# Moving the ranking, the gathered queries and the attention's pace in a two-layer graph transformer

## The chip, the cores and the metric

The kernel runs on one core of a Trainium2 chip. The core has a matmul engine (PE), a vector engine (DVE), a scalar engine (ACT), a general engine (POOL), which here mostly issues gathers and scatters by row number, and SP, which issues plain transfers. Each engine works off its own instructions in order and waits on semaphores for the others. The metric is the device time of one execution, in microseconds (us): the median of several runs.

## The reference

Two layers of a graph transformer work on 2708 nodes with 512 features. Each layer computes, with eight heads of 64:

```python
q, k, v = h @ Wq.T + bq, h @ Wk.T + bk, h @ Wv.T + bv     # (n, 8, 64) each
scores = einsum('nhd,mhd->hnm', q, k) / sqrt(64)
scores = where(mask == 0, -1e9, scores)                    # mask: adjacency plus identity
ctx = einsum('hnm,mhd->nhd', softmax(scores), v)
h1 = layer_norm(h + ctx @ Wo.T + bo)
h2 = layer_norm(h1 + relu(h1 @ W1.T + b1) @ W2.T + b2)     # 2048 hidden features
```

The adjacency matrix is sparse: a node has only a handful of neighbours, so only those scores matter.

## The kernel before, in words

The nodes lie in 22 tiles of 128 rows, the last with 20. The kernel works by edges (`by_edges`): for each node it makes a list of its neighbours, sorts the nodes by the length of their lists ("rank"), and lets attention fetch, for a tile of 128 nodes of like rank, the key and value rows of one neighbour of each by a gather. `CAPS` gives how many neighbours a tile of ranks needs, from 22 for tile 0 down to 7, 6, 5 and 3 for tiles 18 to 21. Attention goes through the tiles in `order`: 21, 20, 19, 18, 8, 9 and so on, short lists first.

**Keys, values and lists (`first`).** For each of the 22 tiles of nodes in their natural order, PE multiplies by Wk and Wv, DVE adds the bias to k (L861), ACT copies v, and ACT's queue writes both to `kv_d` in memory. Beside it, DVE makes the lists from the rows of the adjacency matrix. `counted` then counts, and `ranked` (L738 on) makes each node's rank: four matmuls with a triangle and with ones, two products and sums on DVE, 22 scatters of list records on POOL into `rec_d`, loads of them back in order of rank, and `ident_i`, the node of each rank, for the four last tiles. `ranked` is called behind k of the last tile and ahead of its v (L863).

**Queries (`first_queries`).** For each tile of nodes PE multiplies by Wq; DVE scales and adds the bias into `qs` (L909), and SP writes pairs of tiles to `q_d`. Attention wants queries by rank. For tiles 21, 20 and 19 the kernel doesn't wait for `q_d`: `own_rows` gathers their rows of x by rank (POOL), `turned_own` transposes them (PE, then an ACT copy), and `own_query` multiplies by Wq again (PE, then DVE at L949). Tile 18 and all behind it are gathered out of `q_d` by `asked`, once all of `q_d` is written (`all_made`); until then attention stands still in front of tile 18. `OWN` = 10 says where this happens: after q of tile 9 `listed(True)` makes the gather numbers and the attention's first gathers start, after q of tile 10 come the transposes and the own queries of 21 and 20, after that of tile 12 the own query of 19.

**Attention (`attend`).** A step takes one chunk of two neighbours of a tile: DVE multiplies by q and sums (L1013, L1019), one step later ACT takes the exponential (L1032) and scales one neighbour's values (L1039) while DVE scales the other's and adds (L1045, L1052), and at the tile's end DVE sums and ACT divides into `cx` (L1083). A ring of five buffers (`KVB`) holds gathered chunks. Nothing runs attention by itself: `advance(x)` lets it go on by x chunks, at places in the emitted order; `through(k)` runs it until block k's `cx` is there. `beside_queries` does both during the queries: `advance` of 1.0 or 0.6 for each q behind `OWN`, `through(0)` at the 17th q (NT − 6), and the output projection of block 0 at the 18th.

**Feed-forward.** Blocks of two tiles: transposes of `cx`, the product with Wo (`o`), a norm, transposes of h, and then 16 times a product with W1 (`pf`, L1290), relu on ACT (`ft`, L1298) and, three steps behind, the product with W2 (`a`, L1278). Between these, attention for the next block advances; at step 11 of the first block of layer 0 `through(1)` demands block 1's `cx`. In layer 0 each finished block gets its keys and values for layer 1.

**The border.** Layer 1 starts with 16 queries. Eight have their transposed inputs preloaded (`pool`), the others load `zT` through SP, three at a time. DVE puts each into one of three `qs` buffers and SP writes them to `q_d`. Attention of layer 1 advances by 0.65 of a chunk for each of ten of them (the fifth to the fourteenth); then `through(0)` demands block 0 of layer 1, and the last two queries follow its projection.

**Order.** PE, ACT and SP keep the order in which the code emits their instructions, everywhere. POOL and DVE keep it only within the stretches put by hand (POOL: keys, queries and the first block of layer 0; DVE: queries of layer 0 and the border); elsewhere a planner orders DVE and POOL. `project` puts its result into one of three PSUM buffers named g, or, for `other=True`, into one of three named f.

Of the kernel before, what the change touches and what calls it, by code (L numbers as in the profile page):

```python
# [8 lines left out]
F32 = mybir.dt.float32  # L9
# [9 lines left out]
P = 128  # L19
DM = 512  # L20
# [17 lines left out]
QB = 3  # L38
# [4 lines left out]
XB, XBS = 256, 11  # L43
LEAD = 1.3
QT = 6
OWN = 10
EARLY = 3
FIRST = 4
PACE = (0.62, 0.72)
# [422 lines left out]
def by_edges(ctx: ExitStack, tc: tile.TileContext, x, xT, adj, layers, out, good):  # L472
# [11 lines left out]
    NT = (N + P - 1) // P  # L484
# [20 lines left out]
    own = {}  # L505
    all_made = []
    at = None
# [57 lines left out]
    def project(xs, r, wm, name, other=False):  # L565

        o = (ps_f if other else ps).tile([P, DM], F32, tag="f" if other else "g", name=name)
        for c in range(NC):
            nc.tensor.matmul(o[:r], xs(c), wm[:, c, :], start=(c == 0), stop=(c == NC - 1))  # L569
        return o  # L570
# [243 lines left out]
    def first(w, meanwhile):  # L814

        xg = []

        def load():
            i = len(xg)
            b = i % XBS * XB  # L820
            bw = min(XB, N - b)
            t = wts.tile([P, NC, XB], F32, tag=f"w1_{5 + i % 3}", name="xg")
            xg.append(t)
            step = bw if i else P
            for a in range(0, bw, step):
                nc.sync.dma_start(
                    out=t[:, :, a : a + step], in_=chunked(xT)[:, :, b + a : b + a + step]
                )
                yield

        def tokens(t, again):

            i, c0 = t * P // XB, t * P % XB
            if c0 == 0 and len(xg) < 2 * XBS:
                finish(load())
            xs = xg[i + again * XBS]
            return lambda c: xs[:, c, c0 : c0 + size(t)]

        wk = wts.tile([P, NC, DM], F32, tag="wk", name="wk")
        halves = load()  # L840
        next(halves)
        for c in range(NC):
            nc.sync.dma_start(out=wk[:, c, :], in_=chunked(w["Wk"])[:, c, :])
            if c == 0:
                cols = [given_column(w, "bk")]
        cols.append(given_column(w, "bq"))
        finish(halves)
        turning = turned_row(cols[0], "bk", 1.0)
        bk = next(turning)
        wv = matrix(w, "Wv", "wv")  # L850
        pa = tc.tile_pool(name="pa", bufs=2)
        lists, counted, ranked, listed = lists_of(pa.__enter__())
        done, before = 0, None
        for t in range(NT):
            r = size(t)
            xs = tokens(t, 0)
            kv = wts.tile([P, 2 * DM], F32, tag=f"w2_{5 + t % 3}", name="kvs")
            k = project(xs, r, wk, "k")
            if t == 0:
                finish(turning)  # L860
            nc.vector.tensor_tensor(kv[:r, :DM], k[:r], bk[:r], ALU.add)  # L861
            if t == NT - 1:
                ranked(*counts)  # L863
            v = project(xs, r, wv, "v", other=True)
            nc.scalar.copy(kv[:r, DM:], v[:r])
            if before:
                nc.scalar.dma_start(**before)
            before = dict(out=kv_d[0][t * P : t * P + r, :], in_=kv[:r])
            if t == 0:
                finish(load())  # L870
            while done < min(NT, 1 + LEAD * t):
                lists(done)
                done += 1
                if done == NT:
                    counts = counted()
            meanwhile(t)
            if t == QT:
                wq = matrix(w, "Wq", "wq")
                turning = turned_row(cols[1], "bq", DK**-0.5)
                bq = next(turning)  # L880
                finish(turning)
        nc.scalar.dma_start(**before)
        return bq, wq, listed, pa, tokens

    def first_queries(bq, wq, listed, pa, tokens, meanwhile):

        nonlocal at
        xrs = [own_rows(g) for g in order[:3]]
        made = []

        def written():
            t, qs = made.pop(0)
            if t + 2 < NT:
                out = q_d[0][t * P : (t + 2) * P, :].rearrange("(two p) c -> p two c", p=P)
                nc.sync.dma_start(out=out, in_=qs)
                return
            for i in range(2):
                r = size(t + i)
                nc.sync.dma_start(out=q_d[0][(t + i) * P : (t + i) * P + r, :], in_=qs[:r, i])

        for t in range(NT):
            r = size(t)
            if t % 2 == 0 and made:
                written()
            q = project(tokens(t, 1), r, wq, "q", other=t % 2 > 0)
            if t % 2 == 0:
                qs = wts.tile([P, 2, DM], F32, tag=f"w2_{5 + t // 2 % 3}", name="qs")
                made.append((t, qs))
            nc.vector.scalar_tensor_tensor(  # L909
                qs[:r, t % 2], q[:r], DK**-0.5, bq[:r], ALU.mult, ALU.add  # L910
            )
            if t == OWN - 1:
                listed(True)
                pa.__exit__(None, None, None)
                at = ctx.enter_context(tc.tile_pool(name="at", bufs=2))
                for g in order[:3]:
                    own[g] = at.tile([P, DM], F32, tag="q", name="q", bufs=QB)
                to = dict(own)
                next(ahead)
            if t == OWN:  # L920
                zTs = [turned_own(g, xr) for g, xr in zip(order, xrs)]
                for g, zT in zip(blocks[0], zTs):
                    own_query(g, zT, to[g], bq, wq)
                    advance(0.5)
            if t == OWN + 1:
                listed(False)
            if t == OWN + 2:
                own_query(order[2], zTs[2], to[order[2]], bq, wq)
            meanwhile(t)
        while made:  # L930
            written()
        all_made.append(True)

    def own_rows(g):
        r = size(g)
        xr = dn.tile([P, DM], F32, tag="row", name="xr", bufs=3)
        gather(xr[:r], x, ident_i[:r, g : g + 1])
        return xr

    def turned_own(g, xr):  # L940
        zT = dn.tile([P, NC, P], F32, tag="cT", name="zT", bufs=3)
        flip(xr, size(g), zT[:, :, : size(g)])
        return zT

    def own_query(g, zT, to, bq, wq):

        r = size(g)
        q = project(lambda c: zT[:, c, :r], r, wq, "q")
        nc.vector.scalar_tensor_tensor(to[:r], q[:r], DK**-0.5, bq[:r], ALU.mult, ALU.add)  # L949
# [418 lines left out]
    order = [g for block in blocks for g in block]  # L1368
# [49 lines left out]
    def advance(more):  # L1418

        nonlocal credit  # L1420
        credit = min(credit + more, 1.5)
        while credit > 0 and len(got) < CXB - 1:
            cost = next(ahead, None)
            if cost is None:
                break
            credit -= cost
# [19 lines left out]
    def beside_queries(t):  # L1446

        if t == 3:
            for total, other in sums:
                nc.vector.tensor_tensor(total, total, other, ALU.add)  # L1450
        if len(now.w2) < 5:
            now.load_w1(len(now.w1), nc.scalar)
            now.load_w2(len(now.w2), nc.scalar)
        if t > OWN:
            advance(1.0 if t < NT - 6 else 0.6)
        if t == NT - 6:
            through(0)
            early[0] = now.attended(blocks[0], got)
            next(early[0])
        if t == NT - 5:  # L1460
            for _ in blocks[0]:
                next(early[0])

# [8 lines left out]
    for n in range(NL):  # L1472
        last = n == NL - 1
        nxt = None if last else Layer(n + 1, layers[n + 1])
        if n > 0:
            streamed = now.queries(order[8 : 2 * AHEAD])
            got = {}
            ahead = attend(n, got)
            with tc.manual_schedule(engines={mybir.EngineType.DVE}):
                for _ in range(2):  # L1480
                    now.query(*pool.pop(0))
                next(ahead)
                next(streamed)
                while pool:
                    advance(0.65)
                    now.query(*pool.pop(0))
                for i in range(2 * AHEAD - 10):
                    advance(0.65)
                    next(streamed)
                through(0)  # L1490
                early[n] = now.attended(blocks[0], got)
                next(early[n])
                for _ in blocks[0]:
                    next(early[n])
                finish(streamed)
            now.load_w2(NFC // 2 - 1)
# [141 lines left out]
```

## Time and profile before

| what | value |
|---|---|
| median of three runs | 1971.49 us (1968.82 to 1974.34) |
| the profiled execution, and its span | 1975.51 us, 1973.8 us |
| mean granted clock of PE | 0.985 |
| PE busy | 1902.7 us, 96% |
| DVE busy | 1300.5 us, 66% |
| ACT busy | 933.5 us, 47% |
| POOL busy | 794.1 us, 40% |
| PE's waits for ACT's ft at pf, 3 of them | 9.9 us in all, 6.0 the longest |
| POOL's gathers waiting for DVE's acc | 313.5 us in all |

The profile is of one execution. "Busy" is the time in which an engine has an instruction; the span runs from the first instruction to the last, the execution has 1.7 us around it. Idle time of an engine that is not the bound costs nothing: POOL waits 313.5 us for buffers to come free and nobody need notice. An instruction's line names where it was made; helpers such as `project` (L569) and `gather` (L976) serve many callers, so one goes by the names of the tiles: `kv<-kv_d,idx` is a gathered chunk of attention, `q<-wq,xg` a query, `q<-wq,zT` an own query (layer 0) or a query of the border (layer 1), `tp<-ident,xr` the transposes of gathered rows.

### The profile page before, as it was taken

The numbers are of one execution on the slowest core, as the hardware profiler recorded it, in microseconds if no ns is written. First come the engines' busy times: TensorE is split into PE (matmuls) and PEld (weight loads), VectorE is DVE, ScalarE is ACT, GpSimd is POOL, SyncE is SP. The second block draws the span as 40 slices with busy tenths as digits, with TensorE's granted clock in tenths as the row PEclk, the third lists the DMA queues.
The fourth block names the chain that finished last, engine by engine and source line by source line (L and its number), as shares of the span: only waits on it lengthen the run. The fifth ranks groups of instructions, "written<-read, shape, count | busy, mean of one in ns | idle before, by whom it ended". The sixth has DMA issues, their size and how long they took to land. (4 is left out here: it accounts for less than half of the span.)

```text
span 1973.8 us, 20851 instructions
## 1 busy us (share of the span) xinstructions
PE 1902.7 (96%) x6150; PEld 1102.7 (56%) x6150; DVE 1300.5 (66%) x2141; ACT 933.5 (47%) x3218; POOL 794.1 (40%) x710
## 2 busy tenths in 40 slices
PE   8999989999999999999999998999999999999997
PEld 4443344565656556566566643556666566666664
DVE  6884577684957869558442026887688988877421
ACT  4560244464555655547442112756456765755310
POOL 3114435453645636435210022555346655544210
PEclk9999999999999999999999999999999999999998
DMA  9998667454645647445310646856455766554100
GB/s 331 348 307 286 216 223 258 160 174 166 223 149 190 215 158 237 156 161 187 132 58 22 224 155 231 284 182 215 153 184 192 250 201 221 181 192 148 39 11 13
DMA packets 131487, 366.92 MB, mean 186 GB/s; under 512 B 16669, under 2 KB 36989, under 8 KB 128655
## 3 DMA queue, kind: packets, MB, share of 16 engines
q0 software_dynamic: 69120, 246.35, 37.8%
q1 hardware_dynamic: 53332, 99.66, 14.8%
q10 hardware_dynamic: 8910, 19.48, 2.6%
q8 instruction: 50, 0.82, 0.2%
q14 instruction: 75, 0.61, 0.1%
HBM read 314.62 MB, written 50.83 MB: 185 GB/s over the span
## 5 line engine op out<-in xcount | busy, mean ns | idle before, releaser
L976 POOL DMA_INDIRECT kv<-kv_d,idx x420 | 545.0, 1298 | 475.7 <-DVE acc L1052 313.5
L1278 PE MATMUL a<-w,ft 128*128 128x512 f32 (+1 forms) x1408 | 665.8, 598 | 11.0 <-ACT ft L1298 9.4
L1290 PE MATMUL pf<-hT,w 128*128 128x256 f32 (+1 forms) x2816 | 639.9, 374 | 14.4 <-ACT ft L1298 9.9
L1290 PEld LDWEIGHTS pf<-hT,w 128*128 128x128 f32 x2816 | 523.4, 192 | 193.5 <-issue 106.9
L1278 PEld LDWEIGHTS a<-w,ft 128*128 128x128 f32 (+1 forms) x1408 | 255.8, 186 | 236.6 <-issue 198.7
L1298 ACT ACTIVATE ft<-pf,b 128x256 f32<-128x256 f32 (+1 forms) x352 | 158.5, 459 | 434.0 <-PE pf L1290 433.6
L1013 DVE TENSOR_TENSOR kv<-kv,q 128x1024 f32<-128x1024 f32 (+3 forms) x222 | 256.4, 1158 | 155.0 <-DMA kv<-kv_d,idx 90.3
L1039 ACT ACTIVATE kv<-kv,p 128x64 f32<-128x64 f32 x1232 | 311.0, 334 | 5.0
L1019 DVE TENSOR_REDUCE sc<-kv 128x16 f32<-128x1024 f32 (+3 forms) x222 | 255.0, 1154 | 1.4
L1052 DVE TENSOR_TENSOR acc<-acc,kv 128x1024 f32<-128x1024 f32 (+2 forms) x178 | 203.9, 1146 | 28.7 <-ACT kv L1039 27.9
L1112 POOL TENSOR_TENSOR rd<-va,mhalf 128x1 f32<-128x1 f32 (+1 forms) x88 | 85.2, 968 | 272.2 <-DVE va L1110 270.5
L1032 ACT ACTIVATE p<-sc,minus 128x8 f32<-128x8 f32 (+1 forms) x420 | 103.3, 295 | 154.3 <-DVE sc L1019 154.0
L1045 DVE TENSOR_TENSOR kv<-kv,p 128x512 f32<-128x512 f32 (+1 forms) x178 | 121.5, 683 | 55.8 <-ACT p L1032 55.8
L569 PE MATMUL o<-wo,cT 128*128 128x512 f32 (+1 forms) x352 | 155.1, 593 | 0.5 <-ACT cT L1127 0.5
L569 PEld LDWEIGHTS o<-wo,cT 128*128 128x128 f32 (+1 forms) x352 | 65.1, 186 | 86.5 <-issue 74.5
L1083 ACT ACTIVATE cx<-acc,su 128x64 f32<-128x64 f32 (+1 forms) x352 | 88.4, 333 | 37.8 <-DVE su L1075 31.3
L1310 DVE TENSOR_TENSOR h<-a,h 128x512 f32<-128x512 f32 (+1 forms) x44 | 29.7, 677 | 106.8 <-PE a L1278 106.7
L1116 DVE SCALAR_TENSOR_TENSOR h<-h,rd,ln_b 128x512 f32<-128x512 f32 (+1 forms) x88 | 65.8, 748 | 50.8 <-POOL rd L1112 50.8
L663 ACT ACTIVATE code<-aj 128x2708 bf16<-128x2708 int32 (+1 forms) x22 | 73.3, 3333 | 48.7 <-POOL aj L659 47.4
L666 DVE MAX8 tops<-code 128x8 f32<-128x247 f32 (+2 forms) x242 | 83.1, 400 | 19.2 <-ACT code L663 19.2
L1349 POOL DMA_INDIRECT kv_d<-kvs,ident_i x22 | 23.7, 1078 | 178.7 <-ACT kvs L1343 112.6
L1039 ACT ACTIVATE acc<-kv,p 128x64 f32<-128x64 f32 (+1 forms) x352 | 88.8, 334 | 1.4
(133 smaller groups left out, 1517.0 us busy)
## 6 DMA issues: line engine op xcount, KB each, us to landing
aj<-in_adj SPq DMA_DIRECT2D x21, 1354.0 KB, 7.6
kv_d<-kvs ACTq DMA_DIRECT2D x21, 512.0 KB, 7.0
w<-in_W SPq DMA_DIRECT2D x20, 512.0 KB, 4.7
xg<-in_xT SPq DMA_DIRECT2D x19, 512.0 KB, 8.2
kv<-kv_d,idx POOLq DMA_INDIRECT x420, 5.6
w<-in_W ACTq DMA_DIRECT2D x12, 512.0 KB, 6.0
q_d<-qs SPq DMA_DIRECT2D x22, 256.0 KB, 3.1
zT_d<-zT SPq DMA_DIRECT2D x22, 256.0 KB, 4.8
```

Of the source, the lines that this page charges most:

```text
L569: nc.tensor.matmul(o[:r], xs(c), wm[:, c, :], start=(c == 0), stop=(c == NC - 1))
L976: nc.gpsimd.indirect_dma_start(out=to, out_offset=None, in_=table[:, :], in_offset=bass.IndirectOffsetOnAxis(ap=s, axis=0), bounds_check=N ...
L1013: nc.vector.tensor_tensor(kv[:r, :c, :DM], kv[:r, :c, :DM], self.q[:r].unsqueeze(1).to_broadcast([r, c, DM]), ALU.mult,)
L1019: nc.vector.tensor_reduce(self.sc[:r, s0 : s0 + c, :], kv[:r, :c, :DM].rearrange("p s (h d) -> p s h d", d=DK), AX.X, ALU.add,)
L1032: nc.scalar.activation(p[:r, s, :], self.sc[:r, s, :], AF.Exp, bias=minus[:r, g, s : s + 1])
L1039: nc.scalar.activation(to[:, i, hd], kv[:r, i, DM + h * DK : DM + (h + 1) * DK], AF.Copy, scale=p[:r, s0 + i, h : h + 1],)
L1045: nc.vector.tensor_tensor(to[:, 0, :].rearrange("p (h d) -> p h d", d=DK), kv[:r, 0, DM:].rearrange("p (h d) -> p h d", d=DK), p[:r, s0, : ...
L1052: nc.vector.tensor_tensor(self.acc[:r, :c, :], self.acc[:r, :c, :], kv[:r, :c, DM:], ALU.add)
L1083: nc.scalar.activation(cx[:r, hd], self.acc[:r, 0, hd], AF.Copy, scale=self.su[:r, h : h + 1])
L1278: nc.tensor.matmul(a[:r], fts[f][:, c0 : c0 + r], self.w2[f // 2][:, f % 2, :], start=(f == 0), stop=(f == NFC - 1),)
L1290: nc.tensor.matmul(pf[:, :w], self.w1[f // 2][:, c, f % 2 * P : f % 2 * P + P], hT[:, c, :w], start=(c == 0), stop=(c == NC - 1),)
L1298: nc.scalar.activation(ft[:, :w], pf[:, :w], AF.Relu, bias=self.b1[:, f : f + 1])
```

## The change

Five edits, all in the order of work; what is computed is the same.

- `ranked` is called behind q of tile 0, no longer between k and v of the last tile; the gathers of `own_rows` follow it there.
- `OWN` goes from 10 to 13: the lists' numbers, the first gathers of attention, the transposes and own queries stand three q's later. The own query of tile 19 stands behind q of tile 17 (OWN + 4), not 12 (OWN + 2).
- Tile 18 gets an own query too: its rows are gathered behind q of tile 14, transposed behind q of tile 17, and multiplied behind the last q, into a buffer of its own.
- `through(0)` and the first part of block 0's projection stand at NT − 3 and NT − 2, not at NT − 6 and NT − 5, and the smaller advance of 0.6 starts there.
- At the border attention advances by 0.5 of a chunk for each q, not 0.65.

```diff
-OWN = 10
+OWN = 13
@@ first
-            if t == NT - 1:
-                ranked(*counts)
             v = project(xs, r, wv, "v", other=True)
@@ first_queries
-        xrs = [own_rows(g) for g in order[:3]]
...
             q = project(tokens(t, 1), r, wq, "q", other=t % 2 > 0)
+            if t == 0:
+                ranked(*counts)
+                xrs = [own_rows(g) for g in order[:3]]
...
             if t == OWN + 1:
                 listed(False)
-            if t == OWN + 2:
+                xr = own_rows(order[3])
+            if t == OWN + 4:
                 own_query(order[2], zTs[2], to[order[2]], bq, wq)
+                zT = turned_own(order[3], xr)
             meanwhile(t)
+            if t == NT - 1:
+                g = order[3]
+                own[g] = at.tile([P, DM], F32, tag="q", name="q", bufs=QB)
+                own_query(g, zT, own[g], bq, wq)
@@ beside_queries
         if t > OWN:
-            advance(1.0 if t < NT - 6 else 0.6)
-        if t == NT - 6:
+            advance(1.0 if t < NT - 3 else 0.6)
+        if t == NT - 3:
             through(0)
...
-        if t == NT - 5:
+        if t == NT - 2:
@@ the border
                 while pool:
-                    advance(0.65)
+                    advance(0.5)
                     now.query(*pool.pop(0))
                 for i in range(2 * AHEAD - 10):
-                    advance(0.65)
+                    advance(0.5)
                     next(streamed)
```

More of the change, by code (lines that the diff above doesn't have):

```diff
@@ L882, in first, with first_queries @@
         nc.scalar.dma_start(**before)
-        return bq, wq, listed, pa, tokens
-    def first_queries(bq, wq, listed, pa, tokens, meanwhile):
+        return bq, wq, counts, ranked, listed, pa, tokens
+    def first_queries(bq, wq, counts, ranked, listed, pa, tokens, meanwhile):
         nonlocal at
-        xrs = [own_rows(g) for g in order[:3]]
         made = []
```

## The prediction

> **What bounds the kernel now.** I read the page's busy times and slices, then the timeline of PE in the two stages that the diff touches, then stretches of 5 us for the granted clock, and last the timelines of the queues that feed PE's waits.
>
> ```profile
> span 1973.8 us, 20851 instructions
> PE 1902.7 (96%) x6150; PEld 1102.7 (56%) x6150; DVE 1300.5 (66%) x2141; ACT 933.5 (47%) x3218; POOL 794.1 (40%) x710
> ```
>
> PE works 96% of the span, so time comes out only where PE waits, runs at a lower clock, or does less. The gaps are 1973.8 − 1902.7 = 71 us; the clock's share hides inside the busy time. The largest gaps near the edits, from the timeline of PE (start, length, operation, and in brackets the idle time before it with its releaser):
>
> ```profile
> 162.84 1.22 PE L745 MATMUL pr<-hot,tri 128*128 128x264 f32 x2 [4.34 <-DVE kvs L861]
> ...
> 213.06 1.94 PE L1122 MATMUL tp<-ident,xr 128*128 128x128 f32 x8 [3.89 <-DMA xr<-in_x,ident_i]
> ...
> 287.50 2.34 PE L1290 MATMUL pf<-hT,w 128*128 128x148 f32 x8 [5.97 <-ACT ft L1298]
> ...
> 304.17 2.12 PE L1290 MATMUL pf<-hT,w 128*128 128x148 f32 x8 [2.70 <-ACT ft L1298]
> ...
> 1196.00 7.13 PE L569 MATMUL q<-wq,zT 128*128 128x512 f32 x16 [1.80 <-DVE qs L1220]
> 1204.72 3.70 PE L569 MATMUL q<-wq,zT 128*128 128x512 f32 x8 [1.58 <-DVE qs L1220]
> 1212.34 8.80 PE L569 MATMUL q<-wq,zT 128*128 128x512 f32 x16 [3.92 <-DVE peak L1064]
> ```
>
> The stretches show what a gap costs afterwards. The column ahead of the last two is the clock:
>
> ```profile
> 160.00:165.00 5.00, 2.16 (x5) 1.77 (x6) 3.69 (x15) 0.00 (x0) 0.00 (x0) 0.61 0.59 118
> 165.00:170.00 5.00, 5.00 (x11) 1.55 (x11) 1.87 (x5) 0.00 (x0) 1.55 (x2) 0.71 0.85 303
> ```
>
> At half clock these two lose (0.39 + 0.29) × 5 / 0.5 = 6.8 us of half-speed time. Likewise 6.8 us after the second gap, 6.8 us around the third, 3.4 us after the fourth.
>
> **The skill.** The Trainium skill, "TensorE: Matmul & The Clock Gate", Part 1, says that PE's clock halves after an idle window of about 3.4 us and that windows run free. The trace agrees in size (3.4 and 6.8 us), but gaps of 1.8 and 2.0 us (before 1196 and 381) were followed by no drop and 2.32 us (before 464) by one. The same page, under the array's details, calls ACT and DVE strict first-in-first-out. Here the third gap is that: ft ran at 287.09, behind p and the scalings of the next chunk, though pf for it was done. "DMA: Bandwidth & Descriptors", Anatomy of one DMA, gives a fixed 2.0 us for a gather; rows xr landed here 2.5 to 6.5 us after issue, so I use the trace.
>
> **Rank matmuls behind the first q (L863, before).** Nothing is added; v of the last tile and q of tile 0 go ahead. A 512-wide product of four takes 3.43 us (38.03 us for the 11 at 170.79). k of the last tile ends at 158.4, v at 161.8. q takes a PSUM buffer that DVE frees at L861, at 162.6, the slot that the rank matmuls waited for. So q runs 162.8 to 166.3 after a 1.0 us wait; the rank matmuls follow without a wait, 4 × 0.44 = 1.8 us. PE gains 4.34 − 1.0 = 3.3 us of waiting and about 2.7 us of clock (rank matmuls took 3.8 instead of 1.8, v 4.2 instead of 3.4): 6.0. But ranks are ready 1.5 us later, 169.4 instead of 167.85, and POOL's 22 scatters (1.28 us each), the loads back and the gathers of xr behind them all start 1.5 us later: rows in place at 214.5 instead of 213.06.
>
> **OWN 10 to 13.** Three q's more (10.3 us) stand before the transposes of xr. PE reaches them at 168.0 + 13 × 3.43 + 0.4 = 213.1 and waits 1.4 us instead of 3.89, short enough to keep the clock (before, 3.0 us went there). Own q of tile 21 then ends at 219.3, against 220.6. DVE is the next in line: from 227.7 to 247 it had no gap, with the same list of operations, so the two first results come 1.5 us earlier, 247.2, and PE asks for them at 247.2, against 248.2: hidden, by nothing to spare. Moving `own_query` of tile 19 by two q's costs nothing, since DVE first uses it at 252. `through(0)` moves by three tiles along with OWN, with the same five advances of 1.0 before it.
>
> **The fourth tile.** Added: a gather (1.3 us of POOL, which then had 12.5 us idle until 231.6), four transposes (0.43), an ACT copy (0.59 of an idle stretch), four matmuls (3.43) and a DVE operation (0.6). Removed: one gather out of q_d. So PE does 3.9 us more. In return tile 18's q no longer goes PE, DVE, q_d, gather: DVE began on it at 281.12, 7.5 us after the last q. By PE's order (3.43 each; two q's, two o's, own q, transposes: 20.2 after 247.2, with 1.3 of small waits) block 0's pf starts at 267.9 instead of 275.2. DVE, now with q in place, begins tile 18 at about 273.2 behind the end of tile 19.
>
> From there the chain of attention leads, not PE. From DVE's list at its measured lengths (kv 1.24, sc 1.14, products 0.6, acc 1.13), with one chunk more ahead of the result than before and about 1.2 us for gathers that wait for the ring of five kv buffers, tile 18's sum ends at 296.6 and ACT's eight divisions at 298.6, against 303.8. ft six stands behind them on ACT, so PE waits at pf nine. Replaying pf (1.0) and a (1.93) with ft's places on ACT, I get waits of about 3.3, 1.9, 0.3, 0.8 and 5, with one or two clock drops (1.7 to 4). The transposes of block 1's cx come at 311 instead of 318.03. Then tile 18's norm closes on DVE: it ended at 338.3 as PE asked for it at 337.88; its chunks come 6 us earlier, so PE goes on at 331.5 to 332. **This stage gives 6 us**: the gaps were 17.5 us and the clock some 9, but a chain 6 us earlier is all that can be carried. Both ends: 0 if the gathers wait another 6 us; 12 if the chain keeps up with PE.
>
> Beyond it PE's order is the same and every feeder moves with it, so the 6 us stay.
>
> **The border, 0.65 to 0.5.** Nothing is added; DVE's list changes around the q's of layer 1. A chunk of two costs DVE 1.24 + 1.14 + 0.6 + 1.13 = 4.1 us, 0.65 of one 2.7, with qs 0.67 about 3.3 per q: no room under PE's 3.43. With 0.5 it is 2.7. Between 1190.6 and 1238.1 (47.5 us) PE has 36.1 us of work: eight q's and two o's at 3.43, two pairs of transposes at 0.87. So 11.4 is what the stage holds. In the new list each q's output is taken before the next chunk, so the waits of 1.80 and 1.58 go. The 3.92 us wait is q's input: its zT load stands on SP behind the write of qs, which waited for DVE (1203.99), and landed slowly. It goes too, but the zT of the twelfth q (behind the eighth qs, 1196.6) should still be 1.4 to 2 us late. A new wait: on SP the read of tile 19's q now stands behind one more write, whose qs comes at 1190.2; it is issued at about 1190.6 instead of 1185.76, and DVE wants it at 1194.7. At 4 to 6 us to land it holds DVE up to 2.3 us, and PE about 1.5. **I take 6.5 us**, between 3 and 9. The result of tile 20 comes 2 to 4 us later on DVE, where it had 12 us to spare (1208.9 against 1221.07).
>
> The sum is −12.5 us on the profiled execution (1975.51, span 1973.8 and 1.7 around it), which is 4.0 above the median. On the median of 1971.49: **1959**.
>
> **Rivals.**
> *PE gets all of it.* If attention in layer 0 is never late, the gain there is 17.5 of gaps and 9 of clock, less 3.9 of work and some 4 of waits left, 18, with a border of 8: about 1945. For it: POOL and ACT are idle half of that stage. Against it: DVE ran without a gap from 227.7 to 247.
> *The wait is only moved in layer 0.* Gathers for the ring of five were late by 3.83 us before 308.9 and 3.25 before 322.2; if such a wait falls before tile 18's sum, with a 6.8 us drop of clock, the stage gives 0 and the border 6: 1965.
> *Slower.* The start of attention is bound to its new place: if q of tile 0 is held (its input, or its buffer), the wait of 4.34 stays and the own q's come three q's later, 10.3 us. With 3.9 us of new work, less 6 from the border: 1971.5 + 14.2 − 6 = 1979.7. It decides once own q of tile 21 reaches DVE after about 232 (220.64 now). Against it: q's input was issued at 146.64 and such loads landed in at most 9.5 us.
> *No effect.* The stages cancel, or 0.5 shifts the same waits: 1968 to 1975.
>
> **Chances.** Likeliest (1952 to 1964) 0.62; all of it 0.10; only moved 0.14; no effect 0.08; slower 0.06. What a measurement of this kernel can tell from no change is about 0.3%, 5.9 us: faster is below 1965.6, slower above 1977.4. Faster: 0.62 + 0.10 + about 0.10 of the moved case = 0.82; slower 0.06; the same 0.12. For 8 in 10 I leave out the lower half of "all of it", the slower case and most of no effect: 1948 to 1968.
>
> **What would show it.** Right: no gap over 1.5 us before the first q or the rank matmuls and no drop of clock at 160 to 170; a gap of 1 to 2 us before the transposes of xr at about 214; pf of block 0 starting near 268; tile 18's divisions on ACT ending near 299, with PE's largest gap of the stage just before; the next cx transposes near 311; in the border no gap above 2.5 us and no half clock. Wrong: the xr gap above 3 us, DVE waiting for kv gathers before tile 18's sum, or, in the border, DVE waiting for q of tile 19 by more than 3 us. Later stages giving the 6 us back would show as new ft or acc gaps between 345 and 1000.

## The result and the profile after

| series | kernel before | changed kernel | ratio, 95% interval |
|---|---|---|---|
| first, 15 runs each | 1971.17 us | 1965.27 us (1961.55 to 1969.88) | 0.9970 (0.9959 to 0.9981) |
| later, on a second chip | 1970.94 us | 1966.28 us | 0.9973 (0.9962 to 0.9984) |
| later, on a third chip | 1972.14 us | 1964.43 us | 0.9958 (0.9944 to 0.9971) |

The change saves 5.9, 4.7 and 7.7 us, where 12.5 was forecast. Its profiled execution took 1964.63 us. The head of the page, the kernel after:

```profile
span 1962.9 us, 20872 instructions
PE 1901.0 (97%) x6162; PEld 1100.6 (56%) x6162; DVE 1300.8 (66%) x2142; ACT 933.8 (48%) x3219; POOL 796.8 (41%) x710
```

PE has 12 more matmul records and is busy 1.7 us less; the gaps went from 71 to 62 us. The timeline of PE, same columns as before (start, length, operation, idle time before it with its releaser):

```profile
162.11 3.70 PE L569 MATMUL q<-wq,xg 128*128 128x512 f32 x8 [0.80 <-DVE kvs L861]
165.64 0.61 PE L745 MATMUL pr<-hot,tri 128*128 128x264 f32 x2
...
212.15 1.44 PE L1128 MATMUL tp<-ident,xr 20*128 20x20 f32 x12
...
265.49 4.32 PE L1296 MATMUL pf<-hT,w 128*128 128x148 f32 x32 [0.46 <-ACT hT L1133]
...
277.66 2.34 PE L1296 MATMUL pf<-hT,w 128*128 128x148 f32 x8 [2.81 <-ACT ft L1304]
...
293.35 1.79 PE L1296 MATMUL pf<-hT,w 128*128 128x148 f32 x8 [3.45 <-ACT ft L1304]
...
333.12 1.11 PE L1128 MATMUL tp<-ident,h 128*128 128x128 f32 x4 [3.86 <-DVE h L1122]
...
1189.67 3.70 PE L569 MATMUL q<-wq,zT 128*128 128x512 f32 x8 [1.74 <-DVE qs L1226]
...
1202.15 3.70 PE L569 MATMUL q<-wq,zT 128*128 128x512 f32 x8 [1.21 <-DVE qs L1226]
...
1210.07 6.30 PE L569 MATMUL o<-wo,cT 128*20 128x512 f32 x8 [3.27 <-DVE qs L1226]
```

The waits of 4.34 us (rank matmuls) and 3.89 us (gathered rows) are gone, and block 0's `pf` starts 9.7 us earlier. But the feed-forward of block 0 still waits for attention, and there is a wait of 3.86 us before the second transposes of h that the kernel before did not have. In the border a wait of 3.27 us before `o` stands where 3.92 us stood before a q. The stretches of 5 us around the first q (the column ahead of the last two is the granted clock):

```profile
160.00:165.00 5.00, 4.20 (x11) 1.54 (x9) 3.13 (x10) 0.57 (x1) 0.00 (x0) 1.00 0.49 127
165.00:170.00 5.00, 5.00 (x17) 2.85 (x15) 1.89 (x5) 0.00 (x0) 0.97 (x1) 1.00 1.03 395
```

The clock is full where it was 0.61 and 0.71. Five marks on PE's timeline show how far ahead the changed kernel is along the way:

| mark, us | before | after | difference |
|---|---|---|---|
| first `pf` of block 0 | 275.2 | 265.5 | −9.7 |
| first `pf` of block 1 | 344.3 | 341.6 | −2.7 |
| end of layer 0's last W2 product | 1148.1 | 1138.4 | −9.7 |
| first `pf` of layer 1 | 1238.1 | 1228.9 | −9.2 |
| end of the last W2 product | 1960.4 | 1949.5 | −10.9 |

The stage of layer 0 hands on 2.7 us, not 9.7; the lead grows to 9.7 behind it; the border adds nothing. This pair alone would mislead, though. The records of the granted clock show half-clock windows of 47.6 us in the execution before and 34.0 us in the one after, the last one at the end left out; each costs half of the time in which PE works in it, 20.0 and 14.9 us, so 5.1 us of the lead are windows. (The gaps give 9.2 us more, and 3.4 us go off again for the added work, which is why PE's busy time fell by 1.7 us only.) Some of the windows fall otherwise in other executions. "TensorE: Matmul & The Clock Gate", Part 1, in the Trainium skill says that the windows run free. The runs agree: in each of the twenty profiles the half-clock windows lie on one grid of 3.41 us, which begins elsewhere in each. From 100 us on, a step of that grid at full clock in which PE stood idle for more than 2.0 us was followed by half clock in all of 128 cases, one with 0.5 to 1.3 us in none of 264, and between these in 24 of 145. So a wait of 2 us costs a window or not by where it falls: of six profiles with all edits of layer 0 and the old pace, five have one at the end of layer 0's stage and one has none.

### The profile page after: what moved, and what is told of

It is laid out like the page before. It is cut to its first block, busy times and chain, and to the rows that moved or that the text cites. A ratio compares the mean times of both kernels' runs of the same rounds, so it can differ in the third digit from the quotient of the medians.

```text
span 1962.9 us, 20872 instructions
## 1 busy us (share of the span) xinstructions
PE 1901.0 (97%) x6162; PEld 1100.6 (56%) x6162; DVE 1300.8 (66%) x2142; ACT 933.8 (48%) x3219; POOL 796.8 (41%) x710
## 3 DMA queue, kind: packets, MB, share of 16 engines
q1 hardware_dynamic: 53332, 99.66, 14.9%
```

## The experiments

Each series ran on one chip with its own runs of the kernel before. The letters of the theories are those of each text on record; A and B are named anew in the text of the changed kernel's control. "e1_layer0" in one text is the trial of layer 0 alone. "Border" below is the stretch from the end of layer 0's last W2 product to the first `pf` of layer 1: 90.0 us in both profiles of the kernel before.

**Each half alone.** First the edits of layer 0 without the border's, which is the changed kernel with both of these lines put back:

```diff
-                    advance(0.5)
+                    advance(0.65)
```

and the border's edit alone, which is the kernel before with the reverse.

> The changed kernel with the border's pace put back to 0.65; all of the layer 0 edits stay. Theory A (layer 0 gives the whole gain, the border gives nothing because its old waits are replaced by two new ones): the ratio to the kernel before is that of the changed kernel, 0.997, about 1965 us. Theory B (the border gives its part, layer 0 less): 0.9985 or above, 1968 or more.

> The kernel before with the border's pace at 0.5 and nothing else. Theory A: no change, ratio 0.999 to 1.001 (1969 to 1973 us), with DVE waiting about 3 us for tile 19's q and about 6 us for a write of qs. Theory B: 0.9985 or below, 1968 or less. The recorded prediction's term was 6.5 us: 0.9967.

Measured: 0.9996 (0.9984 to 1.0008) for layer 0 alone, 0.9992 (0.9980 to 1.0004) for the border alone. Neither is told from no change, and 1.2 and 0.7 us do not add up to 5.9. Each theory had one half right: theory A the border (no change, and both of its new waits), theory B layer 0. The border's own profile shows what became of it: its length is 88.6 us, so 1.5 us are gained and not 6.5. First DVE, then PE, of the kernel with the border's edit alone:

```profile
1194.45 1.23 DVE L1013 TENSOR_TENSOR kv<-kv,q 128x1024 f32<-128x1024 f32 x1 [3.07 <-DMA q<-q_d]
...
1215.30 0.69 DVE L1220 SCALAR_TENSOR_TENSOR qs<-q,bq 128x512 f32<-128x512 f32 x1 [5.18 <-DMA q_d<-qs]
```

```profile
1196.38 3.70 PE L569 MATMUL q<-wq,zT 128*128 128x512 f32 x8 [1.70 <-DVE qs L1220]
...
1208.86 3.70 PE L569 MATMUL q<-wq,zT 128*128 128x512 f32 x8 [1.05 <-DVE qs L1220]
...
1216.13 5.07 PE L569 MATMUL o<-wo,cT 128*20 128x512 f32 x8 [2.63 <-DVE qs L1220]
```

DVE now stops twice for transfers: for tile 19's q to come back from memory, and for a `qs` buffer whose write to memory has not landed. PE's `o` needs the PSUM buffer that this `qs` frees.

**Parts of layer 0.** In the same series: the rank matmuls behind the first q alone, on the kernel before (`OWN` stays 10):

```diff
-            if t == NT - 1:
-                ranked(*counts)
@@ first_queries
-        xrs = [own_rows(g) for g in order[:3]]
...
+            if t == 0:
+                ranked(*counts)
+                xrs = [own_rows(g) for g in order[:3]]
```

and all edits of layer 0 but tile 18's own query, so that its q comes out of `q_d` again:

```diff
-                xr = own_rows(order[3])
...
-                zT = turned_own(order[3], xr)
...
-            if t == NT - 1:
-                g = order[3]
-                own[g] = at.tile([P, DM], F32, tag="q", name="q", bufs=QB)
-                own_query(g, zT, own[g], bq, wq)
```

> The kernel before with the rank matmuls and the gathers of own rows behind the first q, OWN still 10, border still 0.65. Theory A (attention's chain from the ranks leads in layer 0): the wait before the rank matmuls turns into a longer one before the transposes of the gathered rows, 3.89 us before and about 9 now, as the rows come 1.5 us later or at the same time; ratio 0.999 to 1.002 (1969 to 1975 us). Rival (PE leads and its waits add up): 6 us less, 0.997.

> The changed kernel's layer 0 without the fourth own query (tile 18 out of the stored queries as before), OWN 13, border 0.65. If the fourth own query carries the gain: DVE starts tile 18 about 7 us after the last q again and the ratio is 0.999 or more. If only DVE's place in its own list matters (it is busy with tile 19 until about 271 anyway): as e1_layer0, 0.997, or 1 to 2 us less for the 3.9 us of PE work saved.

Measured: 1.0007 (0.9996 to 1.0018) and 1.0003 (0.9991 to 1.0016). The rank part alone moves its wait to the next place: with `OWN` = 10, PE stood 7.23 us and again 1.55 us before the transposes of the gathered rows. POOL issued the gathers of these rows 1.0 us later than in the same series' profile of the border alone (203.1 against 202.1). So the forecast's reading that the rows come later (it said 1.5 us), and that `OWN` has to move with it, was right. The kernel with three own queries started block 0's `pf` at 265.7 and the first of block 1 at 341.2, about as the four-tile one does; the fourth tile's worth cannot be told from this.

**The two late transfers of the border.** The next series had the changed kernel once more as a control; the changed kernel with the read of tile 19's q issued by SP behind the first two q's of the border; and that one with every fourth `qs` in a free row buffer of another pool, so that four writes can be under way. (The ring alone was not run.) The early read, and then the fourth buffer:

```diff
                 for _ in range(2):
                     now.query(*pool.pop(0))
+                own[order[2]] = asked(n, order[2])
```

```diff
+            self.turn = 0
...
-            qs = dn.tile([P, DM], F32, tag="row", name="qs", bufs=3)
+            self.turn += 1
+            if self.turn % 4 == 0:
+                qs = rows.tile([P, DM], F32, tag="bo", name="qs")
+            else:
+                qs = dn.tile([P, DM], F32, tag="row", name="qs", bufs=3)
```

> The changed kernel once more, unchanged, beside the others. In the first series its two halves measured 0.9996 and 0.9992 of the kernel before, each within its noise, while the whole had measured 0.997. Theory A (the halves add up and the rest is the luck of where half-clock windows fall): ratio 0.998 to 0.9995, 1965 to 1968 us here. Theory B (the halves need each other: the earlier start of attention makes room that only the slower border pace uses): ratio 0.996 to 0.9975, about 1963 to 1964. In its profile both expect the stage of layer 0 as in the first profile (first pf of block 0 near 265.5, cx transposes of block 1 near 309, the second group of tp h after a wait of 3 to 4 us) and a border of 47 to 48 us from the first q that follows a wait of DVE to the first pf of layer 1; theory A expects half-clock windows in other places than in the first profile.

> The changed kernel with one line more: SP's read of tile 19's q for layer 1 is issued right behind the first two q's of the border, ahead of the writes of later q's. Theory C (the new wait of 3.09 us on DVE for that read is what took the place of the waits that the pace removed): DVE's wait at about 1188 is gone, all of the border's q results come about 3 us earlier, the border is 3 us shorter, ratio to the kernel before 0.0015 lower than that of the changed kernel's control. Theory D (the border is held by the ring of three qs rows, whose write to memory takes 7 us, and the 3.09 us are hidden ahead of that): the border loses less than 1 us, PE's wait of 3.3 us before the o matmul stays or grows by what DVE came earlier.

> The early read of tile 19's q, and every fourth q of layer 1 in another row buffer, so that four instead of three writes can be under way. Theory C: the same as with the early read alone, within 1 us. Theory D: PE's wait before the o matmul (3.27 us on DVE's qs) and the half-clock window behind it go only here: the border is 5 to 6.5 us shorter than in the changed kernel, ratio to the control about 0.997. If neither: the input zT of the last q's is late next (landing about 7 us after issue), the border gains under 2 us and PE shows a wait for zT in the same place.

| kernel | median | ratio | border |
|---|---|---|---|
| changed kernel | 1966.28 us | 0.9973 (0.9962 to 0.9984) | 86.9 us |
| early read of q | 1960.56 us | 0.9948 (0.9932 to 0.9964) | 85.8 us |
| and four buffers for `qs` | 1958.28 us | 0.9929 (0.9916 to 0.9941) | 81.8 us |

So the two transfers are what took the place of the waits that the pace removed. In the changed kernel's first profile, DVE's timeline:

```profile
1187.74 1.23 DVE L1019 TENSOR_TENSOR kv<-kv,q 128x1024 f32<-128x1024 f32 x1 [3.09 <-DMA q<-q_d]
...
1201.47 1.22 DVE L1226 SCALAR_TENSOR_TENSOR qs<-q,bq 128x512 f32<-128x512 f32 x2
...
1202.73 0.67 DVE L1226 SCALAR_TENSOR_TENSOR qs<-q,bq 128x512 f32<-128x512 f32 x1
1209.23 0.69 DVE L1226 SCALAR_TENSOR_TENSOR qs<-q,bq 128x512 f32<-128x512 f32 x1 [5.83 <-DMA q_d<-qs]
```

Three `qs` come within 2 us, so all three buffers are in flight; the fourth waits until the first of them, sent at 1202.13, has landed, some 7 us later. With the early read the first wait is gone; with four buffers the second one too, and all that is left on PE between 1170 and 1228 is this (its waits there, columns: us in total, times, longest):

```profile
PE q L569 <- DMA zT<-zT_d: 1.1, 1, 1.1
PE pf L1301 <- ACT hT L1133: 0.5, 1, 0.5
PE o L569 <- ACT cT L1133: 0.5, 1, 0.5
```

The lengths speak for theory D more than for C: beside the control the early read gains 1.2 us (D asked for under 1), with 2.44 us still waited before `o`, and the buffers another 3.9. A length is of one execution: the other five profiles with this pace and neither fix have 87.5 to 90.5 us, the 90.5 in the changed kernel's first. The 1.2 us are within that spread; the 81.8 us with both, and 81.9 and 82.9 further below, are not. The times of the early read fell by 5.7 us, more than theory C asked for and more than its border shows; which of its executions' waits made that is open. With both, the kernel is 8.0 us below the control. The skill's "Perfetto Trace Analysis", under DMA Instruction — HWDGE, says that a transfer's semaphore waits until its write is confirmed, which can be long where it goes to memory. Agreed: of the border's writes in the changed kernel's first profile, the four whose landing it tells took 3.2 to 7.5 us from issue.

**DVE by hand in layer 0.** In that series also: the changed kernel with DVE too kept in emitted order over layer 0's first FFN block.

```diff
-            in_order.enter_context(tc.manual_schedule(engines={mybir.EngineType.Pool}))
+            in_order.enter_context(
+                tc.manual_schedule(engines={mybir.EngineType.Pool, mybir.EngineType.DVE})
+            )
```

> The changed kernel with DVE too kept in the order of the program over the first FFN block of layer 0, where the planner sets its order in the kernel before and after. Theory E (in layer 0 the end of the stage is set by DVE standing at a kv gather that is late, 4.26 and 4.01 us, ahead of ready work): with products and sums of ready chunks ahead, tile 18's divisions end before 298, PE's wait of 3.86 us before the second tp h is under 2 us, and the stage ends 2 to 4 us earlier (before 331). Theory F (the gathers themselves set the chain, since a gather needs a buffer that only the sum frees): the same sum of waits in other places, the stage ends at 333 to 336 and the time is that of the control within 2 us.

Measured 0.9997 (0.9986 to 1.0008): 3.7 us more than the control. PE's timeline:

```profile
330.02 1.11 PE L1128 MATMUL tp<-ident,h 128*128 128x128 f32 x4 [3.13 <-DVE h L1122]
...
352.14 2.07 PE L1284 MATMUL a<-w,ft 128*128 128x512 f32 x2 [5.24 <-DVE h L1316]
```

The first wait came 3 us earlier, as theory E said, though it still took 3.13 us where E wanted under 2, and a larger one stood behind it. Neither theory had that.

**The missing half.** The control confirmed the changed kernel, so layer 0 had to be worth more than the 1.2 us measured. The next series ran it again, with three more kernels. One is the kernel before with the two diffs above and pace 0.5, so the border alone with both fixes. One is the changed kernel with both fixes and the pace back at 0.65 (the first diff of this section). The last, meant as a better kernel, is the changed kernel with both fixes and DVE by hand for 13 of the 16 steps:

```diff
+        by_hand = ExitStack()
+        if n == 0:
+            by_hand.enter_context(tc.manual_schedule(engines={mybir.EngineType.DVE}))
...
+                if f == 13:
+                    by_hand.close()
```

> The edits of layer 0 alone (border pace left at 0.65) once more, on a chip beside other kernels: the first run of it measured 0.9996 [0.9984, 1.0008] where the kernel before was at 1968.5 us, while the whole change measured 0.997 twice where the kernel before was at 1971. Theory G (the two edits only pay together): 0.9990 to 1.0000 again. Theory H (the first series had the kernel before at a lower time, and layer 0 gives the 5 us that its profile shows from the 20th us of the FFN of layer 0 on): 0.9968 to 0.9982, about 3.5 to 6 us below the kernel before.

> The kernel before with the border alone changed: pace 0.5, and also the early read of tile 19's q and a fourth row buffer for qs. The forecast's border term was 6.5 us (ratio 0.9967), and 0.5 alone measured 0.9992 with a border 1.5 us shorter in its profile. Theory I (the border holds what the forecast said, but the pace alone meets two late transfers): ratio 0.9955 to 0.997, border stage 6.5 to 8.5 us shorter than before. Theory J (the gain of the two fixes needs the earlier layer 0): ratio above 0.998.

> The changed kernel with both fixes of the border, and the border's pace put back from 0.5 to 0.65. Theory K (the pace is what lets each q's output be taken in time, the fixes only make it pay): waits of 1.6 to 2.4 us on DVE's qs before q's come back, the border is 3 to 5 us longer than with 0.5, ratio 0.9945 to 0.9960 against 0.9929. Theory L (the fixes alone are the gain and the pace is worth nothing): within 0.0008 of 0.9929.

> The changed kernel with both fixes of the border, and DVE kept in program order over the first 13 of the 16 steps of layer 0's first FFN block, after which the planner sets its order as in the changed kernel. With DVE in order over the whole block PE's waits for ft fell from 2.81 + 3.45 + 1.38 to 2.93 + 1.95 + 0.73 us and the stage's end came at 330.0 instead of 333.1, but 5.24 us were lost at 352 to a late h of the last tile. Theory M (the loss is the order after the 13th step): the second tp h at about 330, no wait of over 1.5 us at 345 to 360, ratio 0.9912 to 0.9922. Theory N (a sum that is done earlier delays the following tile whatever comes after): a wait of 3 to 5 us on h between 340 and 360 again, ratio 0.993 to 0.995.

| kernel | median (before 1968.42 us) | ratio | border |
|---|---|---|---|
| layer 0 alone, again | 1969.34 us | 1.0004 (0.9992 to 1.0016) | 89.6 us |
| border alone, both fixes | 1959.25 us | 0.9959 (0.9944 to 0.9974) | 81.9 us |
| all, both fixes, pace 0.65 | 1969.87 us | 1.0004 (0.9992 to 1.0015) | 89.3 us |
| all, both fixes, 13 steps by hand | 1963.57 us | 0.9978 (0.9967 to 0.9989) | 82.9 us |

Theory I holds: the border does hold the 6.5 us of the forecast, and more (8.1 us by its length, 9.2 by the medians), but only once the two transfers are out of the way. Pace and fixes need each other, as theory K has it: with 0.65 the fixes give 0.7 us of length, and waits of 1.90, 1.61 and 2.96 us before q's are back (the time is 9 us above what K expected, and layer 0 gives nothing in this series). By hand, neither is right: PE waited 5.61 us before the second transposes of h, which came at 335.8, where M had about 330 and N its wait only between 340 and 360. And layer 0 alone gave nothing again, against theory H, though every profile of it was ahead of the kernel before.

**Three more profiles of layer 0 alone.** The same kernel, profiled three times more on one chip, beside the kernel before.

> A further profiled execution of the edits of layer 0 alone (border pace 0.65), whose median over 14 runs was that of the kernel before twice, while its two profiles showed layer 0 about 4 and 9 us earlier at the 192nd second product of the FFN. Theory P (a wait in the border, which the earlier layer 0 moves into it, varies between executions): spans of 1966 to 1973, with layer 0 as early as in the first profile and 3 us or more lost between 1141 and 1242. Theory Q (layer 0 itself varies, by loads and gathers that land late): the loss lies before 345. Theory R (no wait: the profiles agree, and other executions lose it to half-clock windows in random places): idle of PE within 1 us of the first profile, half-clock windows longer by 6 us or more in sum.

> The same kernel as in the look before, for the spread between executions. Theories P, Q and R expect what they expect there; if all looks are near 1962, the profiles are lower than the other executions for a reason that they don't show.

> The same kernel once more, as in the two looks before, with the same expectations of theories P, Q and R for where its time goes.

> A second profiled execution of the kernel before. The first was 1975.5 us, above its median in every series. If it was an unlucky one, this shows a time near 1968 to 1971, layer 0's first pf at 270 to 274 instead of 275.2 and fewer half-clock windows ahead of it; the gain of layer 0 as read off the first pair of profiles (4.8 to 9.7 us) is then too large by that difference.

These executions took 1964.87, 1974.34 and 1968.65 us, the kernel before 1970.14 us, with its first `pf` at 272.0, where its text had it. The border of the three is 89.0 to 89.8 us: theory P is out. Layer 0's last W2 product ended at 1138.7, 1150.2 and 1143.1. Theory Q is right about the place, for nearly all of the difference lies ahead of 345, but R has the larger half of the amount: of the 11.5 us between the first and the second, 4.2 are idle time of PE and 7.3 the cost of half-clock windows. Where the waits come from is in view. DVE, and then SP, of the second:

```profile
186.15 0.69 DVE L909 SCALAR_TENSOR_TENSOR qs<-q,bq 128x512 f32<-128x512 f32 x1 [2.74 <-PE q L569]
190.98 0.69 DVE L909 SCALAR_TENSOR_TENSOR qs<-q,bq 128x512 f32<-128x512 f32 x1 [4.14 <-PE q L569]
201.48 2.53 DVE L909 SCALAR_TENSOR_TENSOR qs<-q,bq 128x512 f32<-128x512 f32 x4 [9.81 <-remote]
```

```profile
187.34 0.41 SPq L826 DMA_DIRECT2D xg<-in_xT  x1
202.20 0.37 SPq L892 DMA_DIRECT2D q_d<-qs  x1
202.67 0.41 SPq L826 DMA_DIRECT2D xg<-in_xT  x1
```

DVE stands for 9.81 us while POOL issues its scatters; PE meanwhile goes on. The profile names nobody ("remote"), but this `qs` waits for one signal alone, that of PE's matmuls, and the signal is late: by the trace PE's q's ended at 192.98, 196.41 and 199.85, and their signals came at 201.46, 201.55 and 201.64. DVE starts 0.02 us behind the first of them. In the first trial of layer 0 alone the profile does name PE:

```profile
196.13 0.69 DVE L909 SCALAR_TENSOR_TENSOR qs<-q,bq 128x512 f32<-128x512 f32 x1 [6.30 <-PE q L569]
```

The q that it takes ended at 191.32, its signal came at 196.10. In the second of the three profiles SP sends the next write of `qs` only when DVE goes on, and the load of the inputs of the following q's (`xg`), which stands behind it, 15 us after the last. PE waits for it:

```profile
210.45 8.80 PE L569 MATMUL q<-wq,xg 128*128 128x512 f32 x16 [3.74 <-DMA xg<-in_xT]
```

In the changed kernel's first profile DVE's longest idle time between 186 and 204 is 2.74 us, and each of PE's signals there comes within 0.02 us. That separates all twenty profiles, and by the chip of the series, whatever the kernel:

| | first kind of chip (3 series, 8 profiles) | second kind (3 series, 12 profiles) |
|---|---|---|
| DVE's longest idle, 186 to 204 | 2.74 us in all | 6.3 to 10.7 us in all |
| PE's signals of two or three q's within 0.2 us, 186 to 204 | in none | in all |
| medians of the kernel before | 1971.2, 1970.9, 1972.1 | 1968.5, 1968.4 |
| first `pf`, layer 0 as before | 275.2, 274.9 | 272.0, 273.5, 270.7 |
| first `pf`, all edits of layer 0 | 265.4 to 267.2, mean 265.8 | 264.5 to 272.5, mean 267.5 |
| end of layer 0, as before | 1148.1, 1147.3 | 1144.2, 1145.1, 1144.9 |
| end of layer 0, all edits | 1138.4 to 1142.4, mean 1140.1 | 1138.0 to 1150.2, mean 1141.8 |
| gained by the end of layer 0 | 7.6 us | 2.9 us |

(Kernels with parts of the edits or with DVE by hand are left out of the last five rows.) Late signals alone do not make an execution slow: the first of the three, at 1964.87 us, has an idle time of 7.01 us there too. Both trials of layer 0 alone had run on chips of the second kind; the whole had run on the first.

**The whole beside the border alone, on one chip.** This one proved to be of the first kind.

> The changed kernel on one chip with the kernel that has only its border edit. Theory S (layer 0's edits are worth 4 to 5 us beside the slower pace, though nothing without it): ratio 0.996 to 0.9978, and 3 us or more below the border edit alone. Theory T (layer 0's edits are worth some 2 us on average, as the mean of the profiles at the end of its stage shows, and the rest is the scatter of executions and chips): ratio 0.9972 to 0.999, 1 to 3 us below the border edit alone.

> The kernel before with the pace of 0.5 at the border alone, beside the changed kernel on the same chip. It measured 0.9992 before, where theory S expects it again (0.9985 to 1.0000); theory T expects 0.998 to 0.9992.

Measured: 0.9958 (0.9944 to 0.9971) for the whole, 0.9991 (0.9983 to 0.9999) for the border alone. Layer 0 is worth 1970.32 − 1964.43 = 5.9 us there, the border 1.8 us. Theory S is nearest (it had 4 to 5 us for layer 0), but its reason, the pace, is not needed: nothing of layer 0's order differs with the pace, and the kind of chip separates the results as well. I did not run layer 0 alone on a chip of the first kind, nor the whole on one of the second. An estimate from other runs speaks for the chip: on the second kind all with both fixes and DVE by hand took 4.3 us more than the border alone with both fixes, and by hand (there over 16 steps) cost 3.7 us on the first kind; so beside the slow pace too, layer 0's edits gave nothing on the second kind.

## Why the prediction was right or wrong

**The rank matmuls.** Right. PE's wait before the first q was forecast at 1.0 us and measured 0.80; the clock stays full. The four rank matmuls take 1.78 us, from 165.64 to the next q at 167.42, where 1.8 was expected.

**`OWN` and the gathered rows.** Right on the first kind of chip: PE reaches the transposes at 212.15 (forecast 213.1) and waits for nothing, where 1.4 us were expected. On the second kind the premise is missing. There the three profiles with layer 0 as before show at most 0.37 us of waiting for the rows; PE waited 1.0 to 3.1 us for `xg` in front of them, and with the edits it still did, 1.8 and 3.7 us, in two of six executions.

**The fourth tile and the chain of attention.** Mostly right in time: block 0's `pf` at 265.5 (267.9, though the forecast's own 247.2 + 20.2 make 267.4), tile 18's divisions ended at 299.3 (298.6), the next `cx` transposes at 308.8 (311), the second transposes of h at 333.1 (331.5 to 332). Waits of 2.81, 3.45 and 1.38 us on ft came instead of the replayed 3.3, 1.9, 0.3, 0.8 and 5. But then a half-clock window of 6.8 us lay on the end of the stage, and block 1 began only 2.7 us early: the 6 us of this stage did not come there.

**"Beyond it PE's order is the same … so the 6 us stay."** The amount held, the course did not, so that hit is in part luck: 2.7 us at the end of the stage in the first pair, 9.7 at the end of layer 0 (7.6 in the mean of the first kind of chip), 5.9 in the times. Between the two marks of the first pair the kernel before loses more than the changed one, 3.4 us of idle time and 2.9 at half clock, among them waits of 2.01 and 2.32 us at 381 and 464 with a half-clock window behind the second, of which the changed kernel has one, of 1.56 us. On the second kind of chip 2.9 us were left at the end of layer 0, with a standard deviation of 4.5 us between the six profiles with the edits, and nothing in the times. The forecast knew one chip.

**The border: the step that failed.** "I take 6.5 us, between 3 and 9": it gave 1.5 and 1.9 us in length where it stood alone, and 1.8 us in time against the kernel before on the third chip. That is 4.7 of the 6.6 us that the first series missed; the rest is within the intervals of the series. One term was mis-sized and one left out. The new wait, SP's read of tile 19's q behind one more write, was foreseen as "up to 2.3 us" on DVE; in the six profiles with pace 0.5 and neither fix it took 1.84 to 4.03. In the first of them the read was issued about where the forecast had it (1180.83, with 9.7 us of lead) but took 6.9 us to land, where 4 to 6 were taken. The forecast's own signs for this were there in the first profile after: over 3 us of that wait, and a gap over 2.5 us and half clock in the border. And the ring of three `qs` buffers was not in the sum at all, though the profile before had the line on DVE:

```profile
1211.41 0.69 DVE L1220 SCALAR_TENSOR_TENSOR qs<-q,bq 128x512 f32<-128x512 f32 x1 [2.39 <-DMA q_d<-qs]
```

I put the 3.92 us wait down to the late `zT` load and let it go; with q's taken sooner, that write is asked for sooner, DVE waits 4.7 to 5.8 us and PE 2.2 to 3.3 before `o`. The stage held what I counted, 8.1 us with both removed; the edit alone could not get it.

**The sum.** With the measured terms it is 5.9 + 1.8 = 7.7 us on the third chip, the measured difference there, of which these terms are the two parts. Of the rivals, "the wait is only moved in layer 0" gave the nearest time, 1965, with the wrong half: the moved waits are in the border.

## What to carry to other kernels

Before a wait is counted as gain, follow the engine that is to be faster to its next buffer: three buffers, three results in 2 us and a write that lands after 7 us made the next wait. A size read from one execution should be checked on another chip: here DVE stood for up to 10.7 us on one kind under the same code, and the gain of layer 0 could not be measured there. The pace of 0.5 with the early read and four buffers, which beats both kernels (0.9929, 12.7 us), is worth more than the change as made.

## What the runs showed that was not expected

On three of the chips PE's signals reached DVE late while POOL issued its 22 scatters, and DVE stood for 6 to 11 us; on none of the others. The stretches of 5 us, first of the second of the three profiles of layer 0 alone, then of the changed kernel's first (columns after the length: busy PE, weight loads, DVE, ACT, POOL; clock, DMA share, GB/s):

```profile
195.00:200.00 5.00, 5.00 (x13) 2.25 (x12) 0.00 (x0) 0.00 (x0) 2.86 (x3) 1.00 0.07 14
```

```profile
195.00:200.00 5.00, 5.00 (x13) 2.17 (x12) 1.38 (x2) 0.00 (x0) 1.89 (x2) 1.00 0.39 116
```

PE is at full work in both, so the q's that DVE is to take are being made. The DMA queues lie nearly empty while DVE stands, since SP's next transfers wait for it. The skill's "SBUF — State Buffer", SBUF: two separate sides, says that DVE and POOL share a port pair which one instruction can hold to its end. The trace does not show that as the cause: a scatter takes 0.97 us with 0.30 us behind it, so one such hold would not last 9.81 us, and what came late was PE's signal. Many records of signals are missing from the same stretch: of landing DMAs, 193 to 260 stand between 165 and 205 in the profiles of the second kind, 686 to 748 in those of the first, though the packets recorded are as many. Whether the recording of the signals holds them up, or something else does both, no run here tells; nor do I know what the kinds of chip are.

The kernel before is 2.4 to 3.7 us faster on these chips. In the two profiles of it the records of the lists come back sooner there: the later of the two loads that `ident_i` needs was issued at 197.5 and used at 199.9 in its second profile, at 199.3 and 204.1 in its first. That this makes the difference is not shown.
